# Another order for TensorE: a penalty on steps with fresh data, longer planned hand-overs, and five buffer counts, in a four-layer graph network kernel

## The chip, the cores and the metric

The kernel runs on one core of a Trainium2 chip. The metric is the device time of one execution in microseconds (us): the median of three runs for the kernel before. All arithmetic is in float32. One execution was also profiled; every row that is quoted here comes from that one.

## The reference

The input `x` holds 128 batches of 128 nodes with 512 features, `adj` is a 128 x 128 matrix with about 6% of its entries different from zero. Four layers follow each other, and each is closed by `x = layernorm(x + layer(x))`. Cut to what matters:

```python
# layer 0: x @ adj.T, then the maximum over the nodes, plus a bias, relu
# layer 1: attention over the nodes
h   = x @ W                                        # 512 x 512
e   = leaky_relu(s1[:, :, None] + s2[:, None, :]) * adj   # s1 = h @ a1, s2 = h @ a2
hp  = softmax(e) @ h
out = elu(hp + beta * h)
# layer 2: two products
out = (adj @ x) @ weight + bias
# layer 3: eight heads of 64 features, masked where adj == 0
q, k, v = x @ Wq + bq, x @ Wk + bk, x @ Wv + bv
out = softmax(q @ k.T / 8 + mask) @ v
```

No batch needs another one, so 128 chains of four layers run beside each other on one core.

## The kernel before, in words

One batch (a "token" `b` of 128 nodes) is one tile of 128 partitions by 512 columns, and it goes through these steps of TensorE (the names are those in the table `steps` and in `row`):

- `l0`: the product with `adjT` (L424). DVE, ACT and POOL then form the maximum, the relu and the layer norm, and a chain of attention steps ends in `attT`, the turned attention weights. They are turned by way of memory: `att` is written out by a DMA, read back turned, and turned in blocks by DVE (`turn`, L397 to L411).
- `zT` (L559): `x1` times the attention, four products. ACT copies the result out of PSUM (L540).
- `z` (L581): the product with the 512 x 512 weights of layer 1. It is done for two tokens at a time by a scheme with seven block products in place of eight (`pair_products`, `SEVEN`), so it has seven small steps, i = 0 to 6. Steps 2, 3, 4 and 6 read differences of blocks that POOL forms (L550, tiles `Tz` and `Ty`); steps 2, 4 and 5 add to a PSUM bank that ACT must first have copied out (tiles `stz`, `sty`); step 6 adds to the bank "pair" once DVE has finished with what step 4 left there.
- `yT` (L713) and `y` (L581): the same two for layer 2. Here the copy of the bank is followed by a DVE addition of the residual (L752) before the addition that finishes a quarter (L760).
- `q`, `k`, `v` (L888): the three products of layer 3, for four tokens (a group) at a time, again in seven steps each.
- `sc` (L1012): the scores of eight heads. The contraction has 64 rows, so TensorE works in two row tiles, 64*128 in the profile's rows.
- `avT` (L1102): the weights times `v`, in two column tiles, 128*64 in the rows. Before it the softmax weights `pr` (512 KB) go to memory and come back turned into a tile with the tag `pT` (`turn_pr` in the rows), which DVE turns in blocks in place (L407); the tile is held until `avT` has read it.

The last six tokens take a slightly different way (`pT`, `av`) that turns the weights on TensorE.

The order of all this is not written by hand. `Plan.run` (class `Plan`) makes it while the program is built. It keeps a planned clock `now` for TensorE, and at each point looks at the next index of every step. A step is a candidate when its marks (the planned times at which what it reads is ready) have all passed and its buffers are free. Of the candidates it takes the one with the lowest key:

```python
tiled = self.TILED.get(name)
key = ((tiled is None, tiled != mode) if mode else (), place(b))
```

`TILED` names `sc` and `avT`. So while TensorE is in a tiled mode, tiled steps come first, those of the same tiling ahead of the other; otherwise the lowest `place` wins. A place is `(b + turns[name]) * R + row.index(name)` with R = 7 steps in the row: 7 units are one turn, one token. The planned clock goes on by the step's planned cost, plus `SWITCH` = 0.2 us whenever the tiling changes.

What a step sets off on the other engines is a generator. Each `yield` of it names an engine, a planned duration and a rank; the plan puts it in that engine's queue when it is planned to be ready, and the next part is ready `HOP` after the end of that one (`Plan.events`, `self.at(time + us + landing + HOP, gen)`). `HOP` is 0.35 us. When the plan resumes a generator, the code between two yields issues the real instructions. So the same plan fixes the order of the instructions of TensorE, DVE, ACT, POOL and of the DMAs on SP's queue. At run time each engine works through its fixed order and waits with semaphores; nothing is reordered.

Buffers are counted in the plan by tag (`sb_bufs`): `x2` has 5 tiles (the value between layers 1 and 3), `xp` 2 (the residual read back for layer 3), `s2_row` 2 and `att` 1 (layer 1's attention), `pT` 2 (the turned softmax weights). A generator that asks for a tag with none left is parked until one is given back.

Of the kernel before, what the change touches and what calls it, by code (L numbers as in the profile page):

```python
# [16 lines left out]
ALPHA = 0.2  # L17
NEG = -1000000000.0
GB = 4
HOP = 0.35  # L20


class Plan:

# [51 lines left out]
    def events(self, until):  # L78
        while self.heap and self.heap[0][0] <= until:
# [18 lines left out]
            if self.engine.get(engine, 0.0) <= time and self.queue.get(engine):  # L98
                _, _, _, gen, us, landing = heapq.heappop(self.queue[engine])
                self.engine[engine] = time + us  # L100
                self.at(time + us, (None, want))
                self.at(time + us + landing + HOP, gen)
            elif gen is not None and self.engine.get(engine, 0.0) > time:
                self.at(self.engine[engine], (None, want))

    def run(self, steps, total):


        nxt = {name: 0 for name in steps}
        now, mode = 0.0, None  # L110
        while any(nxt[name] < total[name] for name in steps):
            self.events(now)
            best, later = None, []
            for name, (place, cost, waits, bufs, fn) in steps.items():
                b = nxt[name]
                if b >= total[name]:
                    continue
                marks = [self.marks.get(key) for key in waits(b)]
                if any(m is None for m in marks) or any(self.left[t.rstrip("+")] < n for t, n in bufs(b).items()):
                    continue  # L120
                if marks and max(marks) > now:
                    later.append(max(marks))
                else:
                    tiled = self.TILED.get(name)
                    key = ((tiled is None, tiled != mode) if mode else (), place(b))
                    if best is None or key < best[0]:
                        best = (key, name, b)
            if best is None:
                if self.heap:
                    later.append(self.heap[0][0])  # L130
                now = min(later)
                continue
            _, name, b = best
            place, cost, waits, bufs, fn = steps[name]
            nxt[name] += 1
            for tag, n in bufs(b).items():
                if not tag.endswith("+"):
                    self.left[tag] -= n
            now += cost + (self.SWITCH if self.TILED.get(name) != mode else 0.0)
            mode = self.TILED.get(name)  # L140
            self.end = now + HOP
            gen = fn(b)
            self.resume(gen, self.end)
        self.events(float("inf"))
# [3 lines left out]
def kernel(  # L148
# [27 lines left out]


    sb_bufs = {
        "x0": 2, "x1": 5, "x2": 5, "xp": 2,
        "s2_bc": 2, "s2_row": 2, "e": 2, "pe": 2, "att": 1, "attT": 2, "zyT": 2, "Tzy": 1,  # L180
        "xTh": 3, "T": 1, "st": 3, "stzy": 2, "qTh": 3, "kTh": 2, "pr": 2, "pT": 2, "oT": 1,
        "turn1": 2, "turn4": 2,
    }
    ps_bufs = {"mm": 8}
# [40 lines left out]
    x0 = {}  # L225
# [146 lines left out]
    st = [dict() for _ in range(B)]  # L372
# [346 lines left out]
    xTh, xsum, heads = {}, {}, {}  # L719
# [453 lines left out]


    row = ["av", "sc", "yT", "y", "l0", "zT", "z"]
    turns = {'av': 17.5, 'sc': 14.5, 'yT': 5, 'y': 5.25, 'l0': 0, 'zT': 1.5, 'z': 1.5}
    R = len(row)

    def place(name):
        return lambda b: (b + turns[name]) * R + row.index(name)  # L1180
# [76 lines left out]
```

## Time and profile before

| what | value |
|---|---|
| median of 3 runs | 2703.86 us (2703.16 to 2705.64) |
| the profiled execution's own time | 2699.37 us |
| its span, first to last instruction | 2697.3 us |
| granted TensorE clock, mean | 0.994 |
| TensorE (PE) busy | 2601.1 us, 96% of the span |
| weight loads (PEld) busy | 2207.8 us, 82% |
| VectorE (DVE) busy | 2246.2 us, 83% |
| ScalarE (ACT) busy | 1795.9 us, 67% |
| GpSimd (POOL) busy | 1822.0 us, 68% |
| DMA | 425.11 MB, mean 158 GB/s |

The span is 2.1 us shorter than the execution's own time, and that execution is 4.5 us faster than the median. A row of the timeline gives the start, the length, the engine, the line and the operation of merged instructions; ends of matmuls are modelled and overlap the next start, so what a step costs TensorE is the distance from its start to the next step's start.

### The profile page before, as it was taken

What the parts mean: (1) busy time and instruction counts of PE and PEld (TensorE: products, weight loads), DVE (VectorE), ACT (ScalarE), POOL (GpSimd) and SP (SyncE); (2) the same over time, 40 slices, a digit from 0 to 9 for tenths busy, and PEclk for the clock granted to TensorE, in tenths of its full rate; (3) what the DMA queues carried; (4) which work ended last, traced back from release to release, by engine and by line L of the source; (5) the groups of instructions that cost most, each with busy time, mean ns of one, the idle gap of its engine ahead of it and who ended that gap; (6) DMA issues with size and microseconds to landing.
All of it is one profiled execution on the core that took longest, in us unless ns stands there. A gap on an engine that the chain in (4) does not pass through costs nothing. (4 is left out here: it accounts for less than half of the span.)

```text
span 2697.3 us, 48358 instructions
## 1 busy us (share of the span) xinstructions
PE 2601.1 (96%) x15393; PEld 2207.8 (82%) x15393; DVE 2246.2 (83%) x4561; ACT 1795.9 (67%) x4847; POOL 1822.0 (68%) x2664
## 2 busy tenths in 40 slices
PE   6899999999999999999999999999999999999998
PEld 3688878888888888888888888888888888888887
DVE  7579888888888888888888888888888898889876
ACT  4566667566666676666766767676767666667655
POOL 4756667766777667667667676667776667677665
PEclk8999999999999999999999999999999999999999
DMA  5145445555444555545565445654545644455553
GB/s 132 37 122 167 149 149 163 161 187 161 155 154 147 183 164 181 152 144 167 161 186 160 150 141 192 200 165 153 155 154 170 202 148 138 149 172 174 164 176 122
DMA packets 435006, 425.11 MB, mean 158 GB/s; under 512 B 99264, under 2 KB 319552, under 8 KB 434752
## 3 DMA queue, kind: packets, MB, share of 16 engines
q1 hardware_dynamic: 431504, 416.26, 49.7%
q10 hardware_dynamic: 3120, 5.77, 0.8%
q8 instruction: 122, 2.00, 0.3%
q14 instruction: 132, 1.08, 0.1%
q0 software_dynamic: 128, 0.01, 0.0%
HBM read 218.17 MB, written 203.75 MB: 156 GB/s over the span
## 5 line engine op out<-in xcount | busy, mean ns | idle before, releaser
L388 ACT ACTIVATE x<-x,nmr,rstd 128x512 f32<-128x512 f32 x384 | 311.2, 812 | 178.1 <-POOL nmr L386 170.9
L1045 ACT ACTIVATE pr<-pr,nm 128x128 f32<-128x128 f32 x992 | 386.2, 395 | 31.1 <-DVE nm L1040 30.1
L382 POOL TENSOR_SCALAR ve<-mv 128x1 f32<-128x1 f32 x512 | 137.9, 269 | 323.7 <-DVE mv L379 250.0
L384 POOL TENSOR_TENSOR rstd<-ve,nhalf 128x1 f32<-128x1 f32 x512 | 309.8, 605 | 42.6
L377 DVE BATCH_NORM_STATS2 stats<-x 128x6 f32<-128x512 f32 x384 | 259.7, 676 | 25.7 <-ACT x L432 24.7
L440 DVE SCALAR_TENSOR_TENSOR x<-x,wa_bc 128x512 f32<-128x512 f32 x256 | 218.0, 856 | 27.3 <-ACT x L388 26.6
L922 POOL TENSOR_TENSOR st_v<-st_v,bv_bc 128x512 f32<-128x512 f32 x96 | 124.5, 1297 | 138.8 <-ACT st_v L908 137.3
L706 POOL TENSOR_TENSOR x<-x,bias_bc 128x512 f32<-128x512 f32 x128 | 173.5, 1362 | 64.0 <-PE ps_yT L713 41.5
L1128 POOL TENSOR_TENSOR x3r<-turn_o,x3r 128x512 f32<-128x512 f32 x122 | 198.3, 1625 | 20.1 <-DMA x3r<-x_hbm 10.7
L1126 POOL TENSOR_TENSOR turn_o<-turn_o,rd 128x512 f32<-128x512 f32 x122 | 140.0, 1148 | 105.8 <-DVE turn_o L407 89.9
L386 POOL TENSOR_SCALAR nmr<-mv,rstd 128x1 f32<-128x1 f32 x512 | 160.7, 314 | 52.9
L1045 ACT ACTIVATION_READ_ACCUMULATOR pr<-pr,nm 128x1 f32 x976 | 188.7, 193 | 0.0
L407 DVE STREAM_TRANSPOSE turn_pr<-turn_pr 128x1024 f32<-128x1024 f32 x122 | 150.0, 1232 | 31.2 <-DMA turn_pr<-turn_hbm_pr 31.1
L1034 DVE TENSOR_TENSOR pr<-ps_sc,mask 128x512 f32<-128x512 f32 x248 | 162.0, 675 | 14.8 <-PE ps_sc L1012 14.5
L1114 ACT COPY oT<-ps_av 128x512 f32<-128x512 f32 x122 | 132.0, 1082 | 51.9 <-PE ps_av L1102 41.6
L411 DVE STREAM_TRANSPOSE xTh<-turn_x 128x512 f32<-128x512 f32 x124 | 137.5, 1112 | 15.1 <-DMA turn_x<-turn_hbm_x 14.3
L1040 DVE TENSOR_REDUCE nm<-pr 128x8 f32<-128x1024 f32 x124 | 147.7, 1202 | 2.2 <-ACT w_sb L1045 1.9
L559 PEld LDWEIGHTS ps_zT<-attT,x 128*128 128x128 f32 x1024 | 133.3, 192 | 19.4 <-issue 5.8
L424 PE MATMUL psA<-x,adjT 128*128 128x512 f32 x256 | 135.3, 614 | 10.6 <-DMA x<-in_x_dram 9.8
L1012 PEld LDWEIGHTS ps_sc<-kTh,qTh 64*128 64x128 f32 x2048 | 121.8, 187 | 27.1 <-issue 16.0
L388 ACT ACTIVATE x3r<-x3r,nmr,rstd 128x512 f32<-128x512 f32 x122 | 98.7, 812 | 65.9 <-POOL nmr L386 58.7
L559 PE MATMUL ps_zT<-attT,x 128*128 128x128 f32 x1024 | 137.7, 278 | 4.2 <-DVE attT L411 2.3
(198 smaller groups left out, 7666.4 us busy)
## 6 DMA issues: line engine op xcount, KB each, us to landing
turn_hbm_pr<-pr SPq DMA_DIRECT2D x122, 512.0 KB
turn_pr<-turn_hbm_pr SPq DMA_DIRECT2D x122, 512.0 KB
x<-in_x_dram SPq DMA_DIRECT2D x128, 256.0 KB
x3r<-x_hbm SPq DMA_DIRECT2D x128, 256.0 KB
x_hbm<-x SPq DMA_DIRECT2D x124, 256.0 KB
turn_hbm_x<-x SPq DMA_DIRECT2D x124, 256.0 KB
turn_x<-turn_hbm_x SPq DMA_DIRECT2D x124, 256.0 KB
turn_hbm_o<-oT SPq DMA_DIRECT2D x122, 256.0 KB
```

What stands on the lines that cost most here:

```text
L377: nc.vector.bn_stats(stats, src if flat is None else flat)
L384: nc.gpsimd.tensor_tensor(rstd, ve, nhalf, ALU.pow)
L386: nc.gpsimd.tensor_scalar(nmr, mv[:, 0:1], rstd, -1.0, ALU.mult, ALU.mult)
L388: nc.scalar.activation(dst, src, AF.Identity, bias=nmr, scale=rstd)
L407: nc.vector.transpose(t.rearrange("p a n c -> p (a n c)"), t.rearrange("p a n c -> p (a n c)"))
L440: nc.vector.scalar_tensor_tensor(xin_b, x1, 1.0, wa_bc[i], ALU.mult, ALU.mult, accum_out=col)
L559: nc.tensor.matmul(ps[:, c * P : (c + 1) * P], s["x1"][:, c * P : (c + 1) * P], attT, start=True, stop=True)
L706: nc.gpsimd.tensor_tensor(x2, x2, bias2_bc, ALU.add)
L1034: nc.vector.tensor_tensor(pr_h[:, NCC * e : NCC * (e + 1)], pss[e].rearrange("p f (b c) -> p f b c", b=NQ), mask_bc, ALU.add)
L1040: nc.vector.tensor_reduce(nm, pr_h, AX.XY, ALU.max, negate=True)
L1045: nc.scalar.activation(pr_h[:, i], pr_h[:, i], AF.Exp, bias=nm[:, i : i + 1], accum_out=None if late else den[:, i : i + 1])
L1128: nc.gpsimd.tensor_tensor(xp_m, o.rearrange("p a n c -> p a (n c)"), xp_m, ALU.add)
```

## The change

`HOP` goes from 0.35 to 0.45. A candidate whose newest mark is less than `SLACK` = 1.0 us old at the planned time gets `LATEST` = 3.5 added to its place, half a turn, so it is taken only where no candidate with older data stands within half a turn of it. The place of `yT` goes from 5 to 5.5 turns. Five buffer counts change: `x2` 5 to 4, `xp` 2 to 3, `s2_row` 2 to 3, `att` 1 to 2, `pT` 2 to 1. No instruction is added or taken out; the order in which they stand on every engine is another one. The whole diff, but for an empty line:

```diff
-HOP = 0.35
+HOP = 0.45
+SLACK, LATEST = 1.0, 3.5
@@ class Plan, run
-                    key = ((tiled is None, tiled != mode) if mode else (), place(b))
+                    key = ((tiled is None, tiled != mode) if mode else (), place(b) + (LATEST if marks and max(marks) > now - SLACK else 0.0))
@@ sb_bufs
-        "x0": 2, "x1": 5, "x2": 5, "xp": 2,
-        "s2_bc": 2, "s2_row": 2, "e": 2, "pe": 2, "att": 1, "attT": 2, "zyT": 2, "Tzy": 1,
-        "xTh": 3, "T": 1, "st": 3, "stzy": 2, "qTh": 3, "kTh": 2, "pr": 2, "pT": 2, "oT": 1,
+        "x0": 2, "x1": 5, "x2": 4, "xp": 3,
+        "s2_bc": 2, "s2_row": 3, "e": 2, "pe": 2, "att": 2, "attT": 2, "zyT": 2, "Tzy": 1,
+        "xTh": 3, "T": 1, "st": 3, "stzy": 2, "qTh": 3, "kTh": 2, "pr": 2, "pT": 1, "oT": 1,
@@ turns
-    turns = {'av': 17.5, 'sc': 14.5, 'yT': 5, 'y': 5.25, 'l0': 0, 'zT': 1.5, 'z': 1.5}
+    turns = {'av': 17.5, 'sc': 14.5, 'yT': 5.5, 'y': 5.25, 'l0': 0, 'zT': 1.5, 'z': 1.5}
```

## The prediction

> **What bounds the kernel now.** I read the page's busy shares first, then the busy time in three stretches, then the waits of TensorE, then its timeline.
>
> ```profile
> PE 2601.1 (96%) x15393; PEld 2207.8 (82%) x15393; DVE 2246.2 (83%) x4561; ACT 1795.9 (67%) x4847; POOL 1822.0 (68%) x2664
> PE   6899999999999999999999999999999999999998
> ```
>
> TensorE is the bound in nearly all of the span, and it is short of full only at the two ends. DVE at 83% and POOL at 68% matter where TensorE waits for them.
>
> ```profile
> 0.00:120.00 120.00, 85.71 (x321) 54.16 (x322) 77.31 (x183) 54.49 (x115) 69.63 (x99) 0.91 0.39 94
> 120.00:2600.00 2480.00, 2430.45 (x14458) 2078.45 (x14456) 2105.08 (x4262) 1688.30 (x4589) 1703.16 (x2499) 1.00 0.52 161
> 2600.00:2697.00 97.00, 84.94 (x617) 75.19 (x616) 63.84 (x116) 53.15 (x145) 49.23 (x67) 0.95 0.43 144
> ```
>
> In the long middle TensorE (first busy column) is idle for 2480 - 2430.45 = 49.55 us, at a granted clock of 1.00. That is what better order could win, a little more than it by the next but one view. Who ended these waits from 120 to 2650 us (total, times, longest):
>
> ```profile
> PE ps_y_pair L581 <- DVE x L760: 8.4, 9, 2.5
> PE ps_y_pair L581 <- POOL yT L550: 5.0, 6, 1.3
> PE ps_y_chain L581 <- POOL Ty L550: 4.9, 6, 2.7
> PE ps_av L1102 <- DVE turn_pr L407: 2.7, 2, 1.6
> PE ps_zT L559 <- DVE attT L411: 2.1, 3, 1.1
> ```
>
> The small steps of `y` lead: they wait for the addition that frees the bank "pair" and for POOL's block differences. Now the timeline, two places:
>
> ```profile
> 1456.64 1.03 PE L581 MATMUL ps_y_chain<-sums_y,Ty 128*128 128x256 f32 x4
> 1457.50 1.03 PE L581 MATMUL ps_y_pair<-w_sb,yT 128*128 128x256 f32 x4
> 1458.46 1.16 PE L1012 MATMUL ps_sc<-kTh,qTh 64*128 64x128 f32 x16
> 1459.55 1.13 PE L581 MATMUL ps_y_chain<-sums_y,Ty 128*128 128x256 f32 x4
> 1460.52 1.89 PE L888 MATMUL ps_k_chain<-T,sums_k 128*128 128x256 f32 x8
> ...
> 2657.78 3.84 PE L1012 MATMUL ps_sc<-kTh,qTh 64*128 64x128 f32 x64
> 2661.55 1.99 PE L888 MATMUL ps_v_chain<-sums_v,T 128*128 128x256 f32 x8
> ```
> ```profile
> 1187.63 1.03 PE L581 MATMUL ps_y_chain<-sums_y,yT 128*128 128x256 f32 x4
> 1191.55 1.45 PE L581 MATMUL ps_y_pair<-w_sb,Ty 128*128 128x256 f32 x4 [2.89 <-DVE rd L499]
> ```
>
> A `y` step costs 0.86 us start to start (1456.64 to 1457.50), but 0.96 ahead of `sc`, and 0.97 behind it. Four `sc` in a row take 3.77 (2657.78 to 2661.55), one alone 1.09. With c for one `sc` and s for what the stay adds inside it: 4c + s = 3.77 and c + s = 1.09, so c = 0.89 and s = 0.20. The neighbours add 0.10 and 0.11, so a stay costs 0.41 for its two changes of tiling, 0.20 each. The second place shows that a printed wait is too small: 2.89 us are given, but 3.92 - 0.86 = 3.06 are lost, since the modelled end covers the first 0.17. Taking start-to-start distances of all steps less the undisturbed distance of their kind, I find 76 us lost between 120 and 2550 us, 41 of it at `y` (step 6 17, step 3 9, step 2 7), 35 before 120 and under 2 after 2550.
>
> **The change part by part.** No matmul, operation or DMA is added: 7731 matmuls and 1759 DMAs of SP stand in both programs. All is order, so I compare the two orders of TensorE.
>
> *Changes of tiling.* Before, the order holds 94 stays in a tiled mode with 256 changes (rows to columns counts as one). After, 127 stays with 336 changes, because `avT` never follows `avT` with one `pT` tile, and fresh `sc` or `avT` are passed over. 80 x 0.20 = +16 us. The 44 places where `avT` followed `avT` cost 0.05 each by the same distances, and there is none now: -2.2. Sum +13.7, all on TensorE's path, with no cover. The Trainium skill ("TensorEngine Tiling (Array Packing)", Tiling Modes, Key Properties) says that changing the mode drains TensorE, so it speaks against this change; "TensorE: Matmul & The Clock Gate" (Step-by-step: what each phase is for) puts the drain at about 128 cycles, which at its 2.4 GHz is 0.053 us, an estimate of +4 us for 80. The trace's 0.20 is four times that and decides; by the page the total below would be 12 us lower.
>
> *Body stalls.* The plan gives each step an age: its planned start less its newest mark. Sorting the 76 us of loss by the age in the plan of before: `y` steps under 0.1 us old lose 0.53 each (25 of them), 0.1 to 0.25 0.17 (16), 0.25 to 0.5 0.42 (27), 0.5 and more 0.04 (352). Other steps except `z` lose 0.30, 0.19, 0.08 and about 0.02; `z` loses 0.01 at any age. So loss is a matter of planned ages under half a microsecond. The new penalty thins these out little: steps of all kinds under 0.5 us go from 255 to 230, and `y` alone from 72 to 108. The longer `HOP` does more: a `y` step 6 lies four hand-overs behind TensorE (ACT copy, two DVE additions, TensorE), step 3 five, so the same planned age is 0.4 or 0.5 us more real time. The plan costs L752 at 0.42 where the row has 619 ns, so this margin was missing just there. Giving each step of the new order its age plus 0.1 per hand-over, and the loss of that class, I get 25 us for `y` and 50 in all: -26. The bounds: -8 if lateness scatters for `y` as its own steps did (their readiness is spread by about 1 us to both sides of the plan's), which I hold for the low end; -45 if nearly all loss under half a microsecond goes, which no wait excludes. I take -26, since it uses every class as measured.
>
> The order shows the same without ages: of 62 pairs, step 6 of `y` stood less than 4 us of TensorE work behind step 4 in 19; now in 3. But the work between `yT` and step 2 is now under 6 us in 23 pairs (before 5).
>
> *One `pT` tile.* The next `turn_pr` read can only be issued when `avT` is done. The Trainium skill ("Trainium Kernel Development and Optimization", Best Practices) asks for double buffers to overlap DMA and compute, so it too speaks against. Around 1420 us two reads were issued in 1419.89 to 1421.70, and the first transposition began at 1425.29 and took 1.23; where DVE waited for this DMA, 3.6 to 6.4 us lay between issue and transposition. A loop is then some 0.4 + 5.3 + 1.2 + 0.3 = 7.2 us. The new order puts at least 10.1 us of TensorE work between two `avT`, but for four (the lowest 7.6); about 25 stand at 10.2. So the cover is 3 us, and I cost it at nothing; if the loop took 11 us, 25 x 0.8 = 20 us would be lost. SP's queue is in order, so while it waits for `avT` all later DMAs wait too; the plan places the read after `avT`, so that wait should be short.
>
> *Other buffers.* `x2` with 4 delays the start of a token's `z` by one buffer; `att` and `s2_row` let DVE write ahead of the DMA; `xp` lets the residual's read start earlier. None has a wait of TensorE in the table, and their effect is in the order already: zero, with 5 us to both sides. The first 120 us have the same chain of weights and attention: zero, 5 to both sides.
>
> *Tail.* From the last `sc` to the end the new order holds 14.7 us of TensorE work, before 23.6; and the last `pT` is followed by its `av` with nothing between (before 3.7 us). That exposes copies of PSUM (DVE copies of this size have rows near 0.68 us) and softmax work of four tokens: 2 to 8 us, I take +4, against 0.9 lost at the end before.
>
> Sum: 13.7 - 26 + 4 = -8.3 us on the profiled 2699.37, so 2691.1. The median stands 4.5 above that execution: 2703.86 - 8.3 = 2695.6.
>
> **The rivals.** About 0.2% (5.4 us) is what a measurement of this kernel can tell from no change.
>
> *The margin buys only as much as the changes of tiling cost.* Body -18 (between -8 and -26): 13.7 - 18 + 4 = 0, so 2703.6. For it speaks the wide scatter of `y`; against it, that a plan with longer hand-overs also puts DVE's and POOL's operations later, so these block less.
>
> *Slower: block differences late at every turn.* The new order repeats itself every eight tokens, so a late place is late some 14 times. It has 26 steps 2 and 26 steps 3 of `y` with a planned age under 0.3 us (before 13 and 6), all waiting for POOL's L550 behind layer norms of 269 + 605 + 314 ns. If the margin is used up there, each costs 0.53 as the freshest do now: 52 x 0.53 = 28 in place of the 7 counted (13 at 0.42, the rest at 0.04): -8.3 + 21 = +12.7, 2716.6. It turns at 0.29 us lost per step on average, (8.3 + 7) / 52. The `pT` loop at 11 us would give about the same.
>
> *The change does not do what it says*: the count of fresh steps hardly falls, so the penalty itself is nearly idle; that is in the forecast.
>
> **How the numbers follow.** Forecast (faster) 0.48, own range 2683 to 2698; no change 0.22, 2698.5 to 2709; slower 0.30, 2709.3 to 2722. The ends 2682 and 2718 leave out about a tenth on each side.
>
> **What would show it.** In the profile after: about 336 changes of tiling at 0.20 us; the waits of "ps_y_pair" for L760 under 3 us in total; the middle's PE busy time up by some 14 us with its idle time near 30. Wrong would be: waits of `y` for L550 (line moved by 2) of more than 20 us, waits of "ps_av" for the transposition above 10, or more than 10 us idle after the last `sc`. If the changes of tiling cost much under 0.2, the result is below 2690.

## The result: no change that can be measured

The changed kernel takes 2705.82 us (median of 12 runs), the kernel before 2704.2 us (12 runs beside it): a ratio of 1.0006, 95% interval 0.9996 to 1.0016. The forecast was 8.3 us faster, so its sign was not borne out; the range held the time. The likeliest case was wrong, and the rival in which the margin buys as much as the changes of tiling cost had the time right, in part by luck: it had -18 us in the body and +4 in the tail, and they came out at -9.9 and about zero, with -2.7 at the head.

The page of the profiled execution (2700.45 us of its own time), its busy times in two stretches (columns as before, PE busy first), and the waits of TensorE from 120 to 2650 us (total, times, longest):

```profile
span 2698.6 us, 48283 instructions
...
PE 2616.2 (97%) x15393; PEld 2210.1 (82%) x15393; DVE 2250.2 (83%) x4561; ACT 1798.3 (67%) x4847; POOL 1816.9 (67%) x2664
```
```profile
0.00:120.00 120.00, 91.94 (x338) 57.38 (x339) 77.30 (x187) 56.64 (x119) 73.45 (x105) 0.90 0.38 95
120.00:2600.00 2480.00, 2437.76 (x14451) 2077.22 (x14450) 2108.98 (x4257) 1689.81 (x4597) 1692.22 (x2487) 1.00 0.52 161
```
```profile
PE ps_y_pair L583 <- DVE rd L501: 15.7, 10, 3.2
PE ps_y_pair L583 <- POOL yT L552: 13.6, 24, 2.2
PE ps_y_chain L583 <- ACT sty L750: 2.7, 4, 1.0
PE ps_av L1104 <- DVE turn_pr L409: 1.9, 10, 0.2
PE ps_y_chain L583 <- POOL Ty L552: 1.8, 2, 1.2
```

TensorE is busy 15 us longer for the same 15393 records, and its idle time in the middle has fallen only from 49.55 to 42.24 us. The forecast had 30 there. The waits no longer spread over many rows: two rows of "ps_y_pair" hold 29 us, one with 10 waits and one with 24. (Lines are moved by 2 against the kernel before: L762 is the addition that was L760. It adds the bank "pair", which step 3 filled, to a copy of what step 4 left in the bank "chain", and so frees "pair" for step 6.)

The account of TensorE by start-to-start distances, as in the prediction:

| us | before | after | difference | forecast |
|---|---|---|---|---|
| work, with 256 and 336 changes of tiling | 2563.5 | 2577.2 | +13.7 | +13.7 |
| lost before 120 us | 34.9 | 32.2 | -2.7 | 0 |
| lost from 120 to 2550 us | 76.2 | 66.3 | -9.9 | -26 |
| lost after 2550 us | 1.8 | 3.9 | +2.1 | +4 |
| end of TensorE to end of the span | 11.4 | 9.1 | -2.3 | 0 |

With 0.3 us of a later start that is +1.2, and the spans differ by 1.3. One term was badly sized, the third.

**Where the loss is now.** The order of TensorE repeats itself exactly from about 800 to 2500 us: each run of 138 steps (eight tokens, 164 us) is that of 164 us before. In the kernel before, 24% of the steps are the same as 138 steps earlier. From 900 us on nearly all of the loss at `y` (30.5 of 31.9 us) lies at three places of the period: one step 6 (0.5 to 3.4 us each time, 17.3 in ten turns) and two steps 3 (0.57 each time at one, 0.86 or 0.32 at the other). The timeline of the first:

```profile
1447.22 0.42 SPq L403 DMA_DIRECT2D turn_pr<-turn_hbm_pr  x1
1449.43 0.81 ACT L390 ACTIVATE x3r<-x3r,nmr,rstd 128x512 f32<-128x512 f32 x1 [0.44 <-POOL nmr L388]
1450.27 0.34 SPq L1137 DMA_DIRECT2D out_dram<-x3r  x1
...
1451.68 0.52 SPq L403 DMA_DIRECT2D turn_x<-turn_hbm_x  x1
...
1457.09 1.10 DVE L413 STREAM_TRANSPOSE xTh<-turn_x 128x512 f32<-128x512 f32 x1 [1.82 <-DMA turn_x<-turn_hbm_x]
1457.84 1.89 PE L890 MATMUL ps_k_chain<-xTh,sums_k 128*128 128x256 f32 x8
...
1459.94 0.41 DVE L754 TENSOR_TENSOR sty<-sty,x 128x256 f32<-128x256 f32 x1
1460.27 0.68 DVE L934 TENSOR_TENSOR qTh<-ps_q_pair,st_q 128x512 f32<-128x512 f32 x1
1460.87 0.41 DVE L762 TENSOR_TENSOR x<-ps_y_pair,sty 128x256 f32<-128x256 f32 x1
1461.20 0.15 DVE L501 RECIPROCAL rd<-den 128x1 f32<-128x1 f32 x1
...
1461.43 1.10 PE L583 MATMUL ps_y_pair<-w_sb,Ty 128*128 128x256 f32 x4 [1.70 <-DVE rd L501]
```

TensorE loses 1461.43 - 1457.84 - 1.73 = 1.86 us (1.73 is the undisturbed distance of the step of `k` ahead). The row blames the reciprocal L501, which step 6 does not read; what it needs is the addition L762, just ahead of it. That addition is late because DVE stood still for 1.82 us before L413, a transposition for layer 3 whose DMA was issued at 1451.68 and landed only now, and because seven other operations of DVE's fixed queue stand between the two. Period by period, the loss of TensorE, DVE's wait ahead of that transposition, and the time from the issue of its read to its start:

```
loss at y step 6    1.50  1.63  2.01  1.86  1.00  2.68  1.13  0.54  3.36  1.62
DVE's wait at xTh   1.44  1.58  1.95  1.82  0.94  2.81  1.07  0.48  3.31  2.07
issue to start      5.03  5.17  5.55  5.41  5.10  5.97  5.06  4.58  6.93  5.14
```

The plan allows 4.8 us from issue to start (0.35 for the issue, 4.0 for the landing, the hand-over 0.45), so on average only 0.6 us are lost there, though this part makes the difference between one turn and the next. The larger part is that the read is issued late: 2.0 us later on average than the plan has it, measured against the step of TensorE just ahead (1.6 to 2.4 in the ten turns). SP's queue stands still for 1.9 to 2.6 us in each turn, here from 1447.64 to 1450.27, until ACT ends the last layer norm of another token (L390). The DMA of that result (L1137) stands three places ahead of the read. So a wait at the head of SP's queue comes before the one at the head of DVE's; no run moved it.

The granted clock adds to the loss: in the profiled execution it fell to half for 3.4 us behind the two longest of the ten stalls (2.68 and 3.36 us) and behind none of the others there, and the step `zT` that followed lost another 1.6 and 1.5 us. The last column but two is the clock:

```profile
1790.67:1794.09 3.42, 3.42 (x10) 2.71 (x9) 2.45 (x7) 0.81 (x1) 2.74 (x7) 0.50 0.44 115
```

The times of the 12 runs spread over 11.7 us after and over 5.5 us before. The fastest run after had the highest mean clock (0.993), the slowest the lowest (0.989); 0.004 of 2700 us is 11 us, an estimate of what the clock alone makes. That this place causes the spread is not shown: with it mended, 5 runs of one kernel lie within 2.3 us, but 4 of the next one within 7.5.

The second kind, 42 us later in the same period:

```profile
1500.87 1.28 POOL L734 TENSOR_TENSOR T<-xTh,xTh 128x512 f32<-128x512 f32 x1
1501.60 1.13 PE L583 MATMUL ps_y_chain<-sums_y,Ty 128*128 128x256 f32 x4
1502.11 1.25 POOL L552 TENSOR_TENSOR yT<-yT 128x256 f32<-128x256 f32 x1
...
1503.33 1.27 POOL L734 TENSOR_TENSOR T<-xTh,T 128x512 f32<-128x512 f32 x1
1503.42 1.13 PE L583 MATMUL ps_y_pair<-w_sb,yT 128*128 128x256 f32 x4 [0.69 <-POOL yT L552]
```

Step 3 waits for the third difference of `y` (L552), which stands in POOL's queue behind a difference for layer 3 (L734) of 1.27 us. In eight of the ten turns the third difference itself took 1.25 to 1.27 us and step 3 lost 0.85 or 0.86; in two it took 0.72 and step 3 lost 0.31 or 0.32. In all ten it began within 0.012 us of DVE's L442. Where L552 took 0.72, L442 took 1.28, and where L552 took 1.25 and more, L442 took 0.68: each time the longer of the two took nearly the sum of 0.68 and 0.72. So about 0.5 of the 0.86 us goes with this meeting.

### The profile page after: what moved, and what is told of

The parts are those of the page before. It is cut to its first block, busy times and chain, and to the rows that moved or that the text cites. A ratio compares the mean times of both kernels' runs of the same rounds, so it can differ in the third digit from the quotient of the medians.

```text
span 2698.6 us, 48283 instructions
## 1 busy us (share of the span) xinstructions
PE 2616.2 (97%) x15393; PEld 2210.1 (82%) x15393; DVE 2250.2 (83%) x4561; ACT 1798.3 (67%) x4847; POOL 1816.9 (67%) x2664
## 4 chain that ended last, share of the span: by engine, by line
PE 53%; POOL 10%; DVE 9%; DMA 4%; issue 2%; ACT 1%; SPq 0%; POOLq 0%; DVEq 0%; ACTq 0%
PE ps_v_chain L890 6%; PE ps_z_chain L583 6%; PE ps_q_chain L890 5%; PE ps_k_chain L890 4%; PE ps_y_chain L583 3%; PE ps_z_pair L583 3%; PE ps_zT L561 3%; PE ps_y_pair L583 3%; PE ps_k_pair L890 3%; DMA turn_x<-turn_hbm_x 2%; POOL x L708 2%; PE ps_sc L1014 2%; PE ps_av L1104 2%; PE ps_v_pair L890 2%; PE psA L426 2%
## 5 line engine op out<-in xcount | busy, mean ns | idle before, releaser
L390 ACT ACTIVATE x<-x,nmr,rstd 128x512 f32<-128x512 f32 x384 | 311.4, 812 | 126.3 <-POOL nmr L388 92.9
L384 POOL TENSOR_SCALAR ve<-mv 128x1 f32<-128x1 f32 x512 | 145.3, 284 | 342.0 <-DVE mv L381 239.1
L386 POOL TENSOR_TENSOR rstd<-ve,nhalf 128x1 f32<-128x1 f32 x512 | 302.2, 590 | 42.6
L442 DVE SCALAR_TENSOR_TENSOR x<-x,wa_bc 128x512 f32<-128x512 f32 x256 | 213.3, 835 | 14.5 <-ACT x L390 14.2
L1128 POOL TENSOR_TENSOR turn_o<-turn_o,rd 128x512 f32<-128x512 f32 x122 | 130.1, 1067 | 107.9 <-DVE turn_o L409 100.4
L388 POOL TENSOR_SCALAR nmr<-mv,rstd 128x1 f32<-128x1 f32 x512 | 154.2, 301 | 53.0
L552 POOL TENSOR_TENSOR Tz<-zT 128x256 f32<-128x256 f32 x62 | 45.2, 729 | 177.3 <-ACT zT L542 111.6
L413 DVE STREAM_TRANSPOSE xTh<-turn_x 128x512 f32<-128x512 f32 x124 | 137.3, 1110 | 27.7 <-DMA turn_x<-turn_hbm_x 27.3
L715 PEld LDWEIGHTS ps_yT<-adjT,x 128*128 128x128 f32 x1024 | 133.6, 192 | 23.4 <-issue 14.0
L390 ACT ACTIVATE x3r<-x3r,nmr,rstd 128x512 f32<-128x512 f32 x122 | 99.1, 813 | 80.3 <-POOL nmr L388 78.4
L561 PEld LDWEIGHTS ps_zT<-attT,x 128*128 128x128 f32 x1024 | 133.5, 193 | 17.6 <-ACT qTh L915 3.7
```

The lines of the kernel that those rows point to most:

```text
L386: nc.gpsimd.tensor_tensor(rstd, ve, nhalf, ALU.pow)
L390: nc.scalar.activation(dst, src, AF.Identity, bias=nmr, scale=rstd)
L442: nc.vector.scalar_tensor_tensor(xin_b, x1, 1.0, wa_bc[i], ALU.mult, ALU.mult, accum_out=col)
L561: nc.tensor.matmul(ps[:, c * P : (c + 1) * P], s["x1"][:, c * P : (c + 1) * P], attT, start=True, stop=True)
```

## The experiments

Theory A: changes of tiling are paid in full. Theories B and C: the loss is made by the transposition at the head of DVE's queue, and by the T differences in POOL's. Theory D: these places cost because the order repeats them. Theory E: the penalty alone is nearly idle. Ratios are to the kernel before, timed on the same chip, with 95% intervals.

**The buffer counts alone** (the diff is the `sb_bufs` part of the change).

> The kernel before with only the five new buffer counts. Its order has 322 changes of tiling (before 256, after 336) and no avT behind another avT. Theory A, changes of tiling are paid in full on TensorE: 66 x 0.20 - 44 x 0.05 = +11 us of TensorE work, stalls about as before (76 us in the body, give or take 8): about 2715 us. Rival, stays are covered or the buffers free the order by as much: 2704 us or less.

2718.78 us, ratio 1.0049 (1.0036 to 1.0061). TensorE's last matmul ends 17.6 us later: 10.9 us are work by the count of tilings, the rest is loss (body 76 to 89, less 7 at the head). Theory A holds. The changes of tiling come with the buffer counts: 322 with these counts, 281 with the change but the old counts. That it is the single `pT` tile is argued from the plan, which makes 321 changes with that count alone; no run has it alone. By themselves the buffers did not lower the stalls.

**Everything but the buffer counts** (the change, `sb_bufs` as before).

> The changed kernel with the buffer counts of before (hand-over 0.45, penalty and place of yT stay). 281 changes of tiling: +4.8 us of work. Theory A (the single pT tile brings the changes of tiling, the margin lowers the stalls whatever the buffers are): stalls 10 us down as in the changed kernel, 2699 us (2692 to 2706). Rival, the longer hand-overs and the penalty bring nothing of themselves: 2709 us or more.

2716.16 us, ratio 1.0044 (1.0029 to 1.0058): the rival. The body loses 70 us, 6 less than before, but the work is 4.8 us more and the last 150 us lose 24 in place of 2, with `q` waiting there for T and for `xTh`. My 2699 took no account of the tail.

**The transposition later in DVE's queue.** TensorE's order and the plan's times are untouched; the real instruction is issued up to 2 us later by the plan's clock, or as soon as a reader or the next user of its tile is issued. (The diffs from here on are cut to the lines that matter.)

```diff
-        nc.vector.transpose(dst, t)
+        if n == NCC:
+            put_off(off_x, 2.0, lambda: nc.vector.transpose(dst, t))
+        else:
+            nc.vector.transpose(dst, t)
```

> The changed kernel with TensorE's order and every planned time as they are; only DVE's transposition of the layer-3 input (into xTh) is issued up to 2 us later in DVE's queue, so at the recurring place 3 instead of 8 DVE operations stand between it and the addition that frees the bank for y step 6. Theory B (step 6 loses 1 to 3.4 us there every eight tokens because this transposition waits for its DMA at the head of DVE's queue): the loss at y step 6 falls from 21 to below 8 us, total 2705.8 - 13 = 2693 us. Rival, the additions are late by themselves or the DMA holds something else up: loss stays near 20 us, 2704 us or more.

2692.59 us, ratio 0.9953 (0.9940 to 0.9967). Loss at `y` step 6 fell from 21.2 to 5.9 us, at step 3 it stayed (17.9 and 20.1). The row of L501 is gone from the top of TensorE's waits (lines are moved again, L576 is the difference of `y`, L525 the reciprocal):

```profile
PE ps_y_pair L607 <- POOL yT L576: 15.5, 24, 2.2
PE ps_zT L585 <- DVE rd L525: 4.6, 7, 1.6
PE ps_y_chain L607 <- ACT sty L775: 2.8, 4, 1.0
```

The recurring place, with only two operations left between the transposition (L435) and the addition (L787):

```profile
1454.30 1.10 DVE L435 STREAM_TRANSPOSE xTh<-turn_x 128x512 f32<-128x512 f32 x1
1455.24 0.41 DVE L779 TENSOR_TENSOR sty<-sty,x 128x256 f32<-128x256 f32 x1
1455.57 0.68 DVE L964 TENSOR_TENSOR qTh<-ps_q_pair,st_q 128x512 f32<-128x512 f32 x1
1456.16 0.42 DVE L787 TENSOR_TENSOR x<-ps_y_pair,sty 128x256 f32<-128x256 f32 x1
...
1456.72 1.10 PE L607 MATMUL ps_y_pair<-w_sb,Ty 128*128 128x256 f32 x4
```

In nine of the ten turns DVE no longer waits there (0.02 us at most) and step 6 loses 0.04 to 0.33 us; in the tenth DVE waits 1.05 and step 6 loses 1.20. Theory B holds: no work was taken away; 48 of the 124 transpositions stand 1 to 5 places further back in DVE's queue, the ten at this place 5. In this profiled execution 6 us of the gain were lost again behind 2666 us, where the granted clock stood at 0.50.

**Both put off** (transposition by up to 4 us, in place of 2 in the run above, T differences by up to 2).

```diff
-            nc.gpsimd.tensor_tensor(dst, x_, y_, ALU.subtract)
+            put_off(off_T, 2.0, lambda dst=dst, x_=x_, y_=y_: (flush(off_x), nc.gpsimd.tensor_tensor(dst, x_, y_, ALU.subtract)))
```

> As the last one, and POOL's four block differences of a group of tokens (tile T, line 734 of the changed kernel) are issued up to 2 us later in POOL's queue, each behind one more of y's differences; TensorE's order and all planned times as they are. Theory C (y step 3 loses 0.6 and 0.9 us at two recurring places because its third difference stands behind a T difference of 1.3 us): loss at y step 3 falls from 18 to below 6 us, total about 2683 us. Rival, the layer norms ahead of them on POOL are what is late, or q and k now wait for T: loss at y step 3 or at q and k stays above 12 us, 2692 us or more.

2677.98 us, ratio 0.9900 (0.9885 to 0.9916). POOL's queue at the two places of the period, read from the built programs (Y a difference of `y`, T one of layer 3, n a layer norm, b the bias addition):

```
after         ...bnbYnYnTYTYTnTnn...   ...bnbbnTYTYTYTYnnnn...
both put off  ...bnbYnYnYTYTnTnTn...   ...bnbbnYTYTYTYnTnnn...
```

At both places one T fewer stands ahead of the third Y. At the second place the meeting with DVE's L442 is gone as well, but the 1.27 us of the T difference are by themselves more than the 0.86 that were lost. Loss at step 3 fell to 6.0 us, and TensorE's waits from 120 to 2650 us have no large row left:

```profile
PE ps_y_pair L607 <- POOL yT L576: 4.7, 3, 2.2
PE ps_y_chain L607 <- POOL Ty L576: 3.7, 3, 1.8
PE ps_y_pair L607 <- DVE rd L1084: 3.6, 6, 1.2
PE ps_av L1133 <- DVE turn_pr L430: 3.5, 12, 0.7
```

**Only the T differences put off.**

> The changed kernel with only POOL's T differences put up to 2 us later in POOL's queue; the transposition stays where it is, TensorE's order too. Theory C: loss at y step 3 falls from 18 to about 6 us, at y step 6 it stays near 20: 2705.8 - 12 = 2694 us. Rival, the two places hang together (the relief of POOL lets step 6 go too, or one stall only moves to the other): 2682 us or less, or 2702 us or more.

2689.75 us, ratio 0.9944 (0.9931 to 0.9957). Step 3 falls to 5.6 us, step 6 stays at 23.8. So the two kinds of place are independent, and their gains add within what the runs can tell: 13 and 16 us singly, 28 together, each uncertain by some 3 to 4 us by the intervals. Theory C holds.

**The put-offs in the kernel before** (both by up to 2 us).

> The kernel before with the same two put-offs (transposition into xTh and T differences up to 2 us later in their queues), TensorE's order of before. Theory D (the repairs work on places that the regular order of the change makes recur; the order of before meets them only here and there): y step 6 from 17 to 10 and y step 3 from 9 to 7 us, about 2695 us. Rival, the late operations cost the order of before as much, so the change itself brings nothing: 2682 us or less. Other rival, they don't matter there: 2702 us or more.

2710.54 us, ratio 1.0022 (1.0013 to 1.0030): slower. Step 6 went from 17.3 to 15.5 us, but step 3 from 8.7 to 10.4 and step 2 from 7.1 to 12.4. Of the expectations the other rival came, that the put-offs don't matter there, and they even cost 6 us; theory D had expected a gain of 9. What is left of it is that they pay in the repeating order and not in this one. I read it so that in an order without repetition an operation put off comes to stand ahead of an urgent one about as often as behind it; that was not traced place by place.

**The hand-overs alone** (`HOP = 0.45`).

> The kernel before with only the planned hand-over 0.45. 297 changes of tiling: +7.8 us of work. If the margin alone lowers the loss at y steps (step 6 from 17 to 8): about 2706 us. From the run with all but the buffers (2716), where the tail was 20 us longer, I hold a longer tail for likely here too: 2712 us (2704 to 2720).

2711.77 us, ratio 1.0026 (1.0014 to 1.0038). The margin does what it was counted for at `y` (step 6 from 17.3 to 11.1, step 3 from 8.7 to 3.7), but the whole body falls only from 76 to 71, against 7.8 us of work and 10 more lost in the tail.

**The penalty alone** (`SLACK`, `LATEST` and the new key).

> The kernel before with only the penalty of half a turn on fresh steps. 246 changes of tiling: -1.9 us of work. Theory E (the penalty alone is nearly idle: y step 6 stands less than 4 us behind step 4 in 16 pairs in place of 19): 2706 us (2700 to 2712). Rival, the penalty is what lowers the stalls: 2695 us or less.

2723.58 us, ratio 1.0070 (1.0058 to 1.0082). Theory E fails: I had held the penalty for idle, and it costs 19 us. The body loses 104 us in place of 76: step 6 less (13.9), but `y` step 5 goes from 4.0 to 13.9, `avT` from 5 to 12, `zT` from 5 to 11. That a step passed over for half a turn makes its own followers late is my reading; the trace shows only where the loss is.

**Put-offs (both by up to 2 us), and no penalty on `sc` and `avT`.**

```diff
-place(b) + (LATEST if marks and max(marks) > now - SLACK else 0.0))
+place(b) + (LATEST if name not in self.TILED and marks and max(marks) > now - SLACK else 0.0))
```

> Both put-offs, and the penalty is no longer laid on sc and avT (it had no effect on TensorE's order in the body: the order is the same up to the last 50 steps). Only the tail is another one, with 3 changes of tiling less. Theory: 3 x 0.20 = 0.6 us of work less and up to 3 us less waiting after 2600 us, so 2675 us (2672 to 2678). Rival, the tail is set by the softmax and layer norm chains of the last tokens: no change, 2678 us.

2672.83 us, ratio 0.9878 (0.9863 to 0.9893): the best of all, 1.2% ahead of the kernel before and, by the medians, of the changed one. Its advantage over the kernel with both put-offs was not measured side by side, the intervals overlap, and the transposition's put-off differs too (2 us here, 4 there); the loss after 2550 us fell from 3.9 to 3.0 us. The middle of its profile, with 25.8 us idle:

```profile
120.00:2600.00 2480.00, 2454.20 (x14636) 2102.06 (x14635) 2139.46 (x4289) 1700.02 (x4639) 1698.30 (x2504) 1.00 0.53 163
```

**Without the penalty, with and without the put-offs** (`LATEST = 0.0`).

> Both put-offs, but the penalty on fresh steps is zero (hand-over 0.45, place of yT, buffers as in the changed kernel). Its order of TensorE does not repeat itself every eight tokens (29% of the steps are as one period earlier, 84% with the penalty) and has 327 changes of tiling, 1.8 us of work less. Theory D (the put-offs pay because the places recur, and the penalty is what makes them recur): 2700 us (2692 to 2712). Rival (buffers and hand-overs would do as well): 2682 us or less.

> The changed kernel with the penalty at zero and nothing put off: TensorE's order is that of the last run (no repetition). Theory D, strict form (put-offs pay only where places recur): as the last run, 2689 us (2684 to 2695). Rival (the transposition and the T differences stand in the way in this order too, at changing places): the put-offs were worth 10 us or more, so 2699 us or more.

2689.44 us, ratio 0.9949 (0.9933 to 0.9965), and 2689.04 us, ratio 0.9943 (0.9931 to 0.9955). The put-offs are worth nothing in this order, as theory D says, and the expectation of 2700 for the first was too high. The second says more: the change without its penalty is 15 us faster than before. TensorE loses 57.1 us in its body there, against 66.3 with the penalty and 76.2 before, and has 9 changes of tiling fewer than with it. These two make 11 us, which is what the spans of the profiled executions differ by (2698.6 and 2687.7); the medians differ by 17. The middle, with 36.2 us idle:

```profile
120.00:2600.00 2480.00, 2443.82 (x14498) 2084.78 (x14498) 2106.71 (x4269) 1696.22 (x4604) 1702.08 (x2498) 1.00 0.53 162
```

## Why the prediction was right or wrong

*Changes of tiling, +13.7: right.* In the changed kernel's trace a `y` step costs 0.863 us, 0.957 ahead of a tiled step and 0.967 behind one, the same to 0.001 as before. The estimate of 0.053 us, from the drain of about 128 cycles in the Trainium skill ("TensorE: Matmul & The Clock Gate", Step-by-step: what each phase is for), would have left the account above 12 us short of the last matmul's end.

*One `pT` tile costs nothing at its loop: right.* The waits of "ps_av" are 10 of at most 0.2 us. Its real price is the tilings that it separates.

*Tail, +4: right in kind.* TensorE lost 3.9 us there, most of it 2.05 us at one `av` behind its `pT` copy; the end behind it became 2.3 shorter, which I had not counted.

*Body stalls, -26: this step failed.* It gave every step of the new order the mean loss of its class of age. That is an average over places that come up once each; the new order comes by the same few places ten times and more. The recurring step 6 has a planned age of 0.50 us, with the margin 0.9: its class loses 0.04 us a time, and it lost 1.7 on average, since the transposition ahead began 2.6 us later than planned (2.0 of them at SP's queue). No age of the step itself shows that, for what is late is another operation ahead of its producer in DVE's queue. This place alone is 17 us, about the size of the miss: -9.9 in place of -26. The classes had a warning in them: "a matter of planned ages under half a microsecond" leaves out 352 x 0.04 = 14 of the 41 us at `y`, lost by older steps. The low end of the forecast's own bounds, -8 if lateness scatters for `y` as its own steps did, was near the measured -9.9.

*The slower rival: its mechanism came, at other sizes.* It named late places at every turn among steps 2 and 3 of `y` behind POOL. Step 3 went from 9 to 18 us as it said, but behind T differences and not layer norms; step 2 fell from 7 to 2; and the largest place was step 6, behind DVE, which it did not name.

*That the penalty is nearly idle: wrong.* The counts of fresh steps were right and said little. With the other edits the penalty costs 17 us (2705.8 against 2689.0), alone 19. None of the orders without it repeats: between 900 and 2500 us of the plan's clock 97% of the steps in the changed kernel bear the name of the step one period earlier, and 29% without the penalty. But the penalty alone doesn't make it repeat: with everything but the buffer counts the share is 24%, as in the kernel before. With the two places mended the repeating order is the better one by 11 us and more. Why a repeating order comes out of just this combination stays open.

*What the runs leave open.* The place of `yT` was not run alone, nor was any one of the five buffer counts, nor a move of the DMA that holds SP's queue up. The edits do not add: apart they cost 14 (buffers), 7 (hand-overs) and 19 us (penalty), together 2, so a price for each edit by itself does not exist here.

## What to carry to other kernels

An engine whose queue is in order makes everything behind its head late, so look for the wait at the head (here a transposition for another layer that waits for a DMA, whose issue in turn stood behind a wait at the head of SP's queue), not for the instruction that the row names. Where a planner makes an order that repeats, a late place is paid at every turn: list the losses by their place in the period, since two kinds of instruction put off by 2 to 4 us were then worth 28 us. And price an edit to a planner on the whole order that comes out of it, changes of tiling counted, because the edits' effects neither add nor keep their sign.

## What the runs showed of the hardware that was not expected

A change of tiling cost the same 0.20 us in each of the three traces where I took it (before, after, both put off), whatever stood around it. A printed wait of TensorE is short by about 0.17 us, so 49.55 us of idle time were 76 us of loss. From the issue of the read of a `turn_x` tile to DVE's start on it lay 3.3 to 5.9 us in the changed kernel (5% to 95% of the 23 cases in which DVE waited over 0.15 us), and at the recurring place (4.6 to 6.9) that spread went straight into TensorE's loss. There stalls of 2.7 and 3.4 us were followed by 3.4 us at half the clock, those of up to 2.0 us were not. POOL's differences and DVE's L442, begun within 0.012 us of each other, took 0.72 and 1.28 us, or 1.25 and 0.68, but never both the short time.
